# One layer of two attentions and two rotation blocks: earlier loads in the prologue, shared coupling products, a wider output projection

## The chip, the cores and the metric

The kernel runs on one core of a Trainium2 chip. The metric is the device time of one execution in microseconds (us); the time shown for the kernel before is the median of three runs. The engines are PE (TensorE), DVE (VectorE), ACT (ScalarE), POOL (GpSimd) and SP (SyncE, which here only issues DMAs). Each engine works through its own queue in order.

## What is computed

The input `x` is 2 batches of 2048 tokens with 256 features, all in float32. Four residual steps follow each other, each on the layer norm of what came before:

```python
x = x + attn_a(layernorm(x))   # 16 query heads of 16, 4 key heads, softmax over 2048 keys, projection Wo, bias bo
x = x + ffn(layernorm(x))
x = x + attn_b(layernorm(x))   # linear attention with a causal mask, rotary positions and a gate
x = x + ffn(layernorm(x))
```

The `ffn` is three cycles of a rotation, whose strength a small network computes for each token:

```python
gf = global_net(x.mean(axis=1))                    # one number for each batch
for _ in range(3):
    tf = sigmoid(gelu(gelu(gelu(out @ w1 + b1) @ w2 + b2) @ w3 + b3) @ w4 + b4)   # 256 -> 256 -> 128 -> 64 -> 1
    coupling = 0.1 + adaptive_range * (0.7 * gf + 0.3 * tf - 0.5) * 2.0
    out = out + coupling * twist(out)              # twist: [p_r, -p_i, -o_r, o_i] of the four quarters
```

## The kernel before

The 4096 tokens are eight blocks of 512 (`BLK`), four for each batch. `xs` holds all tokens with the tokens on the partitions; `zq` holds features on the partitions.

**Prologue of attention a** (lines 487 to 606). `arrive(j)` (L251) asks on SP's queue for block j of `x`. `look(j)` (L262) takes its statistics on DVE and its scale on POOL; `spread(j)` (L282) normalizes it, some of its four token tiles on DVE and the rest on ACT; `features(j)` (L293) turns it on PE and evacuates the two halves by DVE or ACT, as its argument says; `keys(j)` (L306) projects keys and values (`pk`), splits the keys into a rounded part and a rest (`kh`, `kl`), writes both to DRAM (`dk`, L244) and fetches them back spread over the partitions (`a_kP`, L249); `values(j)` (L322) turns the values (`pv`); `asked(j, m)` (L333) projects queries (`pq`); `project(u)` (L349) sends the queries of unit u through DRAM in the same way (`dq`, `qP`). `biases` (L196) gathers the key and query biases with small matmuls. `WARM` idle matmuls stand at the start.

**The maxima.** A unit is a block of queries and one of four groups, 32 in all. The generator `largest` (L362) finds each query's largest score: a step is one score matmul `s` (L376) and one DVE reduction `mx` (L380), 64 steps to a unit. After a unit's last step four small DVE operations build a row (`mr`), which goes to DRAM and back on SP's queue (`dm`, L398, then `a_m`, L403). The prologue runs the first `LEAD` = 80 steps, between which the pieces of work for the remaining blocks stand: one piece at each third step (`pieces`, L572; 22 pieces and an end). The tiles `s` have three PSUM banks of their own; in unit 0 some use the four banks of the pool `p`, which pieces and scores use too.

**The loop** (L617) has 512 iterations of a unit and 128 keys: four scores `p` (L625), four matmuls that add the maximum's row (L629, "shift"), four exponentials on ACT (L633), four `av` matmuls of the iteration before (L612), and four steps of `largest`. `finish(u)` (L445) is a generator that brings a unit's result through DRAM to `oc` in small steps; after a block's last group it projects it, one token tile at a time (`po`, L483), and adds it to `xs` (L484). `norm(j)` (L410) normalizes and turns blocks 0 to 2 for the first rotation within the loop.

**Order.** A scheduler may rearrange the instructions of an engine where no dependency forbids it. `in_order` (L136) pins the program's order on the engines that it is given: on all five for the prologue (L606), and again for everything behind attention a (L1362). The loop between is not pinned.

**Rotations** (L742). Blocks go in pairs k (12 pairs: three cycles of four): `first(k, e)` is the layer `q1` of block e of the pair, `second(k)` is `q2`, `third(k)` is `q3` (one block on each half of the partitions), `fourth(k)` applies the rotation. In the last cycle (k of 8 and more) `fourth` calls `back` (L831): the couplings are computed with the tokens on the partitions (`q4`, L839, eight matmuls with one column each; then `cf`, L844 to L846, once for each block), the features are turned (`trf`, L858), added to `xs` (L862), and the rotation's products are added too (L870); in the second rotation each half block is then stored. `rounds` (L1161) interleaves neighbouring pairs.

Of the kernel before, what the change touches and what calls it, by code (L numbers as in the profile page):

```python
# [67 lines left out]
def tile_hybrid(ctx: ExitStack, tc: tile.TileContext, x: bass.AP, consts: bass.AP, wa_d: bass.AP, wf_d: bass.AP, wb_d: bass.AP, out: bass.AP):  # L68
# [84 lines left out]
    def attention_a():  # L153
        with ExitStack() as st:
# [26 lines left out]
            def bank(name):  # L181
                return banks[0](name)
# [13 lines left out]
            def biases(raw, at, bqr, sel):  # L196


                pb = psp.tile([P, BLK], F32, tag="p", name="a_pbias")
                rows, bv = sel[:, 0:64], sel[0:1, 64:P]  # L200
                compact(rows, ident, nc.scalar.copy)
                compact(bv, raw[0:1, at["bv"][0] : at["bv"][1]], nc.scalar.copy)
                mm(pb[0:64, 0:1], rows, raw[:, at["bk"][0] : at["bk"][1]], start=True, stop=True)
                mm(pb[64:P, 0:1], bv, ones[0:1, 0:1], start=True, stop=True)
                pq = psp.tile([P, BLK], F32, tag="p", name="a_pbq")
                for e in range(2):
                    mm(pq[64 * e : 64 * e + 64, 0:2], rows, bqr[:, e::2], start=True, stop=True)
                nc.vector.tensor_copy(bkv, pb[:, 0:1])
                nc.vector.tensor_copy(bq, pq[:, 0:2])
# [52 lines left out]
            def look(j):  # L262

                st = own.tile([P, 4, 6], F32, tag="ln_st", name=f"st_a{j}", bufs=4)
                mv = own.tile([P, 4, 2], F32, tag="ln_mv", name=f"mv_a{j}", bufs=4)
                rs, nb = (own.tile([P, 4], F32, tag=f"ln_{t}", name=f"{t}_a{j}", bufs=4) for t in ("rs", "nb"))
                for t in range(4):
                    if t == 3:
                        yield
                    nc.vector.bn_stats(st[:, t, :], xs[:, 4 * j + t, :])  # L270
# [139 lines left out]
            def norm(j):  # L410

                zt = later_pools["late"].tile([P, 4, D], F32, tag="zt", name=f"zt0_{j}")
                yield from normalize_slowly(zt, j)
                if j == 2:
                    first_norms.append(zt)
                    return
                for c in range(2):
                    yield
# [26 lines left out]
            def finish(u, av):  # L445
# [60 lines left out]
            arrive(2)  # L506
            arrive(3)
# [23 lines left out]
            list(two)  # L531
# [3 lines left out]
            list(three)  # L535
            first()
            second = keys(1, ld)
            second()
            arrive(BPB)
# [7 lines left out]
            third()  # L547
            next(ahead)
# [6 lines left out]
            project(1)()  # L555
            nc.sync.dma_start(small[:, P : _CONST["ones"][0]], consts[:, P : _CONST["ones"][0]])
# [3 lines left out]
            for j in range(BPB + 1, NB):  # L560
                arrive(j)
# [10 lines left out]
            def pieces():  # L572

                memsets()
                list(look(4))
# [8 lines left out]
                for j in range(BPB, NB):  # L584
                    features(j, ld, 0)
                    if j + 1 < NB:
                        list(look(j + 1))
# [29 lines left out]
            for u, kb in ((u, kb) for u in range(len(units)) for kb in range(KB)):  # L617
                qP, mrow = queries[u], mrows[u % 2]
# [80 lines left out]
    def behind(tail):  # L699
# [41 lines left out]

        def rotations(n, part, store):  # L742
            alphas, plains = {}, {}
            acts, narrow = {}, {}
# [32 lines left out]
            def first(k, e):  # L777
# [3 lines left out]
                for m in range(2):  # L781
                    q1 = bank(f"q1f{n}_{k}_{e}_{m}")
# [5 lines left out]
            def second(k):  # L788
                narrow[k] = []
                for e in range(2):  # L790
# [6 lines left out]
                    narrow[k].append(a2)  # L797

# [31 lines left out]

            def back(k, js, a3, between):  # L831


                both = []
                for e in range(2):
                    row = slice(64 * e, 64 * e + 64)
                    q4 = bank(f"q4f{n}_{k}_{e}")
                    for tile in range(4):
                        mm(  # L839
                            q4[:, tile : tile + 1], a3[row, tile * P : (tile + 1) * P], w4[row, 0:1],  # L840
                            start=True, stop=True,
                        )
                    tt = take("small", [P, 3, 4], f"cf{n}_{k}_{e}")
                    nc.scalar.activation(tt[:, 2, :], q4[:, 0:4], AF.Tanh, bias=hb4, scale=0.5)  # L844
                    nc.vector.tensor_scalar(tt[:, 0, :], tt[:, 2, :], plain, plains[js[e] // BPB], ALU.mult, ALU.add)
                    nc.vector.tensor_scalar(tt[:, 1, :], tt[:, 0, :], -1.0, None, ALU.mult)  # L846
                    both.append(tt)
                for e in range(2):
                    j, cs, z = js[e], both[e], blk(zq, js[e])
                    if e == 1 and between:  # L850
                        between()
                    for h in range(2):
                        tr = bank(f"trf{n}_{k}_{e}_{h}")
                        for q in range(2):
                            at = slice((2 * h + q) * P, (2 * h + q + 1) * P)
                            for c in range(2):
                                to = q * D + (1 - c) * P
                                nc.tensor.transpose(tr[:, to : to + P], z[:, c, at], ident)  # L858
                        tr = tr.rearrange("p (q s f) -> p q s f", q=2, s=2)
                        half = tokens(j)[:, 2 * h : 2 * h + 2, :].rearrange("p q (s f) -> p q s f", s=2)  # L860
                        for s in range(2):
                            nc.vector.tensor_tensor(half[:, :, s, :], half[:, :, s, :], tr[:, :, 1 - s, :], ALU.add)  # L862
                        for q in range(2):
# [5 lines left out]
                            for m, quarters in enumerate((slice(0, 4, 3), slice(1, 3))):  # L869
                                nc.vector.scalar_tensor_tensor(  # L870
                                    x4[:, quarters, :], t4[:, quarters, :], cs[:, m, tile : tile + 1],
# [9 lines left out]
            return context, first, second, third, fourth  # L881
# [279 lines left out]
        def rounds(f, n):  # L1161

            context, first, second, third, fourth = f
# [15 lines left out]
        context, first, second, third, fourth = f  # L1179
# [97 lines left out]
        context, first, second, third, fourth = f  # L1277
# [82 lines left out]
        for n in range(8, 27):  # L1360
            rounds(f, n)
        in_order(begin)  # L1362
# [119 lines left out]
```

## Time and profile before

| what | value |
|---|---|
| median of three runs | 2176.52 us (2175.12 to 2176.97) |
| the profiled execution, its time | 2173.25 us |
| its span, first to last instruction | 2171.5 us |
| mean granted clock of PE | 0.992 of full |
| prologue: first `s`, first `av` of the loop | 28.99 us, 114.36 us |
| the loop, first to last `av` | 114.36 to 1554 us |
| first rotation, with the seam to attention b | 1554 to 1742 us |
| attention b and the second rotation up to its last cycle | 1742 to 2119 us |
| last DVE product, end of span | 2168.4 us, 2171.5 us |

The page of a profile lists the busy time of each engine, and the chain of work that ended last, followed back from the last instruction. A timeline lists instructions in order of time, merged: start, duration, engine, line, operation, output and inputs, and in square brackets the engine's idle time before, with what ended it. A table by stretches gives each engine's busy time and, behind the engines, the granted clock (PEclk, 1.00 is full speed), the DMA engines' busy share and GB/s. Fp32 matmuls appear as two records ("passes") each.

### The profile page before, as it was taken

How to read it: one execution, taken by the hardware profiler on the slowest of the kernel's cores; microseconds unless marked ns; L12 is line 12 of the kernel's file. 1: busy time of each engine (PE TensorE's matmuls, PEld its weight loads, DVE VectorE, ACT ScalarE, POOL GpSimd, SP SyncE). 2: the span in 40 equal slices, each digit the busy share in tenths (PEclk: the TensorE clock that was granted, in tenths of full speed). 3: DMA queues.
4: the chain of work that ended last, by engine and by line, in shares of the span. 5: the costliest groups of instructions: out<-in, count | busy, mean ns of one | idle time of the engine just before them, and what ended most of it. 6: DMA issues, size and time to landing. Idle time of an engine off the chain costs nothing.

```text
span 2171.5 us, 38896 instructions
## 1 busy us (share of the span) xinstructions
PE 2120.0 (98%) x14218; PEld 1019.6 (47%) x14218; DVE 1730.8 (80%) x3351; ACT 1417.8 (65%) x2748; POOL 348.8 (16%) x318
## 2 busy tenths in 40 slices
PE   8899999999999999999999999999999999999998
PEld 3344444444444444444444444444443567676334
DVE  5899998998999899899899899987144688876435
ACT  3377777777776777777677677778864445454442
POOL 3100000000001000000000000000145345541550
PEclk9999999999999999999999999999999999999999
DMA  6510110101101011010110101100100000000002
GB/s 179 146 54 15 40 36 17 46 12 46 36 17 46 10 48 36 17 46 12 47 36 17 37 19 48 36 17 7 51 1 0 1 1 2 1 2 1 0 1 78
DMA packets 59696, 68.73 MB, mean 32 GB/s; under 512 B 24944, under 2 KB 34032, under 8 KB 59248
## 3 DMA queue, kind: packets, MB, share of 16 engines
q1 hardware_dynamic: 58592, 64.79, 10.9%
q8 instruction: 112, 1.84, 0.3%
q10 hardware_dynamic: 720, 0.92, 0.1%
q14 instruction: 80, 0.66, 0.1%
q0 software_dynamic: 192, 0.52, 0.1%
HBM read 35.78 MB, written 26.21 MB: 29 GB/s over the span
## 4 chain that ended last, share of the span: by engine, by line
PE 85%; DVE 9%; DMA 2%; ACT 2%; issue 1%; SPq 1%; POOL 1%; ACTq 0%; DVEq 0%; POOLq 0%
PE av L612 21%; PE s L376 19%; PE p L625 10%; PE q1f L784 8%; PE p L629 6%; DVE mx L380 6%; PE q2f L794 4%; PE pe L1072 2%; PE po L483 2%; PE bpo L1098 1%; PE pv L942 1%; PE pw L942 1%; PE pq L933 1%; PE q3f L804 1%; PE pk L933 1%
## 5 line engine op out<-in xcount | busy, mean ns | idle before, releaser
L380 DVE TENSOR_REDUCE mx<-s 128x1 f32<-128x512 f32 x2048 | 1270.6, 681 | 104.1 <-PE s L376 102.5
L633 ACT ACTIVATE e<-p 128x512 f32<-128x512 f32 x2048 | 1058.8, 603 | 362.2 <-PE p L629 347.1
L376 PE MATMUL s<-a_kP,qP 64*128 64x512 f32 x2048 | 709.6, 471 | 26.9 <-DVE mx L380 24.4
L629 PE MATMUL p<-a_m,a_pick 64*128 64x512 f32 x2048 | 591.5, 416 | 0.0
L376 PEld LDWEIGHTS s<-a_kP,qP 64*128 64x128 f32 x2048 | 283.9, 184 | 588.9 <-DVE mx L380 563.4
L612 PE MATMUL av<-e,a_v 128*32 128x512 f32 x4096 | 547.2, 606 | 0.0
L625 PE MATMUL p<-qP,a_kP 64*128 64x512 f32 x2048 | 528.9, 393 | 2.0 <-ACT e L633 2.0
L625 PEld LDWEIGHTS p<-qP,a_kP 64*128 64x128 f32 x2048 | 286.4, 185 | 61.5 <-ACT e L633 26.4
L629 PEld LDWEIGHTS p<-a_m,a_pick 64*128 64x128 f32 x2048 | 283.8, 184 | 27.7
L477 POOL TENSOR_TENSOR oc<-oc,sums 128x512 f32<-128x512 f32 x16 | 20.9, 1304 | 1226.1 <-DMA sums<-dr 1078.2
L784 PE MATMUL q1f<-zq,wf 128*128 128x512 f32 x384 | 175.5, 600 | 0.0
L612 PEld LDWEIGHTS av<-e,a_v 128*32 128x32 f32 x4096 | 81.1, 108 | 129.3 <-issue 120.6
L785 ACT ACTIVATE a1f<-q1f,wf 128x512 f32<-128x512 f32 x96 | 65.8, 687 | 99.8 <-PE q1f L784 96.4
L784 PEld LDWEIGHTS q1f<-zq,wf 128*128 128x128 f32 x384 | 70.6, 190 | 98.0 <-issue 85.5
L794 PE MATMUL q2f<-a1f,wf 128*128 128x512 f32 x192 | 89.6, 610 | 0.0
L1078 DVE TENSOR_TENSOR en<-pe,small 128x512 f32<-128x512 f32 x128 | 79.3, 681 | 12.8 <-PE pe L1072 12.6
L823 DVE TENSOR_SCALAR cf<-cf,f_beta,alphaf 128x512 f32<-128x512 f32 x32 | 33.6, 1050 | 53.8 <-ACT cf L822 53.8
L827 POOL TENSOR_TENSOR tf<-cf,zq 128x512 f32<-128x512 f32 x32 | 55.5, 1735 | 92.1 <-DVE cf L823 91.7
L796 ACT ACTIVATE a2f<-q2f,wf 128x512 f32<-128x512 f32 x48 | 32.7, 686 | 55.0 <-PE q2f L794 55.0
L829 POOL TENSOR_TENSOR zq<-zq,tf 128x512 f32<-128x512 f32 x32 | 56.8, 1774 | 3.1 <-DVE tf L826 0.7
L794 PEld LDWEIGHTS q2f<-a1f,wf 128*128 128x128 f32 x192 | 35.2, 193 | 45.3 <-issue 44.4
L828 DVE TENSOR_TENSOR zq<-zq,tf 128x512 f32<-128x512 f32 x32 | 22.1, 692 | 36.1 <-POOL tf L827 36.0
(205 smaller groups left out, 1634.9 us busy)
## 6 DMA issues: line engine op xcount, KB each, us to landing
qP<-dq SPq DMA_DIRECT2D x64, 256.0 KB
dq<-qh SPq DMA_DIRECT2D x62, 128.0 KB
dq<-ql SPq DMA_DIRECT2D x62, 128.0 KB
a_kP<-dk SPq DMA_DIRECT2D x16, 256.0 KB
oc<-avs SPq DMA_DIRECT2D x128, 32.0 KB
sums<-dr SPq DMA_DIRECT2D x128, 32.0 KB
out<-xs SPq DMA_DIRECT2D x16, 256.0 KB
xs<-in_x SPq DMA_DIRECT2D x7, 512.0 KB
```

Of the source, the lines that this page charges most:

```text
L376: mm(s, qP[r // 2][row, qi * P : (qi + 1) * P], kP[r // 2][row, k0 + kb * BLK : k0 + (kb + 1) * BLK], start=True, stop=True,)
L380: nc.vector.tensor_reduce(mx[:, r, qi : qi + 1, kb], s, AX.X, ALU.max)
L612: mm(av[32 * r : 32 * r + 32, :], vA[:, units[u][0] // BPB * KB + kb, 32 * r : 32 * r + 32], es[r], start=(kb == 0), stop=(kb == KB - 1),)
L625: mm(t[r], kP[r // 2][row, k0 : k0 + P], qP[r // 2][row, :], start=True, stop=False)
L629: mm(t[r], pick[row, :], mrow[r // 2][row, :], start=False, stop=True)
L633: nc.scalar.activation(es[r], t[r], AF.Exp, scale=1.0 / HD**0.5)
L784: mm(q1, w1[:, c, m * P : (m + 1) * P], z[:, c, :], start=(c == 0), stop=(c == 1))
L785: nc.scalar.activation(a1[:, m, :], q1, AF.Gelu, bias=b1[:, m : m + 1])
L794: mm(q2, w2[:, c, :], a1[:, c, :], start=(c == 0), stop=(c == 1))
L827: nc.gpsimd.tensor_tensor(t1, cs, z[:, 0, :], ALU.mult)
L829: nc.gpsimd.tensor_tensor(z[:, 1, :], z[:, 1, :], t1, ALU.subtract)
L1078: nc.vector.tensor_tensor(self.ens[t][w], pes[w].rearrange("p (h n) -> p h n", h=4), const("triu").unsqueeze(1).to_broadcast([P, 4, P]), A ...
```

## The change

It edits these places:

- Loads: blocks 2, 3 and 4 are asked for at the start instead of 2 and 3; block 5 after the fetch of the first queries, block 6 after the fetch of block 2's keys, block 7 after the second unit's queries. Before, block 4 came after block 1's keys and 5 to 7 after two loads of constants.
- Start: six idle matmuls instead of four; the biases' matmuls and copies move behind block 0's normalization, block 0's two halves are both evacuated by ACT, and `look` is no longer split.
- `LEAD` is 74, and six more steps (`MORE`) stand in the loop's first twelve iterations, one in each second. The pieces stand at each third step up to step 52, none from 53 to 63, and the last five at steps 64 to 72.
- PE's order is pinned from the prologue through the loop's iteration (0, 3); the other four engines as before.
- The projection takes two token tiles into one PSUM bank and adds 512 columns at once. `norm` turns both halves of a block in one step.
- In `back` one set of four matmuls with two columns (`w4_pair`, zero where the other block's rows are) gives the couplings of both blocks of a pair, with one tanh and one pair of scalings.
- At the very end pair 10's `fourth` stands between the two halves of `first(11, 1)`, and pair 11's turns and plain additions behind each half of `second(11)`; `fourth(11)` then only adds the products.

```diff
+                yield
...
-                    if t == 3:
-                        yield
...
+                yield
                 for c in range(2):
-                    yield
                     tr = bank(f"ztr0_{j}_{c}")
...
-                    for t in range(4):
-                        po = bank(f"po{j}_{t}")
-                        for h in range(2):
-                            mm(po[:, 0:D], oc[:, h, t * P : (t + 1) * P], wo[:, h, :], start=(h == 0), stop=(h == 1))
-                        nc.vector.tensor_tensor(xs[:, 4 * j + t, :], xs[:, 4 * j + t, :], po[:, 0:D], ALU.add)
+                    for i in range(2):
+                        po = bank(f"po{j}_{i}")
+                        for t in range(2):
+                            tok = slice((2 * i + t) * P, (2 * i + t + 1) * P)
+                            for h in range(2):
+                                mm(
+                                    po[:, t * D : (t + 1) * D], oc[:, h, tok], wo[:, h, :],
+                                    start=(h == 0), stop=(h == 1),
+                                )
+                        pair = tokens(j)[:, 2 * i : 2 * i + 2, :]
+                        nc.vector.tensor_tensor(pair, pair, po.rearrange("p (t d) -> p t d", t=2), ALU.add)
                         yield
...
-            LEAD, WARM = 64 + 16, 4
+            LEAD, MORE, WARM = 64 + 10, 6, 6
...
-            arrive(2)
-            arrive(3)
+            for j in range(2, 5):
+                arrive(j)
...
-            list(look(0))
-            biases(raw, at, bqr, sel)
-            one, two, three = look(1), look(2), look(3)
-            next(one)
+            look(0)
+            picked = biases(raw, at, bqr, sel)
+            next(picked)
             spread(0, ld, 2)
-            next(one)
-            features(0, ld, 1)
+            features(0, ld, 0)
+            look(1)
+            next(picked, None)
...
             first()
+            arrive(5)
             second = keys(1, ld)
             second()
-            arrive(BPB)
...
             third()
+            arrive(6)
...
             project(1)()
+            arrive(7)
...
-            for j in range(BPB + 1, NB):
-                arrive(j)
...
-                if n % 3 == 1:
+                if (n % 3 == 1 and n < 55) or (n > 63 and n % 2 == 0):
                     next(rest, None)
-            in_order(begin, (engines.PE, engines.DVE, engines.Activation, engines.Pool, engines.SP))
+            in_order(begin, (engines.DVE, engines.Activation, engines.Pool, engines.SP))
...
+                if (u, kb) == (0, 4):
+                    in_order(begin, (engines.PE,))
...
+                if kb % 2 == 1 and u * KB + kb < 2 * MORE:
+                    next(ahead)
...
+            def turn_ahead(k, e):
+                for h in range(2):
+                    turned[k, e, h] = turn_back(k, e, h)
...
+                q4 = bank(f"q4f{n}_{k}")
+                for tile in range(4):
+                    mm(
+                        q4[:, 2 * tile : 2 * tile + 2], a3[:, tile * P : (tile + 1) * P], w4_pair,
+                        start=True, stop=True,
+                    )
+                cs = take("small", [P, 3, 8], f"cf{n}_{k}")
+                nc.scalar.activation(cs[:, 2, :], q4[:, 0:8], AF.Tanh, bias=hb4, scale=0.5)
+                nc.vector.tensor_scalar(cs[:, 0, :], cs[:, 2, :], plain, plains[js[0] // BPB], ALU.mult, ALU.add)
+                nc.vector.tensor_scalar(cs[:, 1, :], cs[:, 0, :], -1.0, None, ALU.mult)
...
+                        half, tr = turned.pop((k, e, h), None) or turn_back(k, e, h)
...
-        for n in range(8, 27):
+        for n in range(8, 23):
             rounds(f, n)
+        third(10)
+        first(11, 1, lambda: fourth(10))
+        second(11, lambda e: turn_ahead(11, e))
+        third(11)
+        fourth(11)
```

`turn_back` is the old body of `back`'s inner loop up to the two additions of L862: four transposes into a bank and two DVE additions.

More of the change, by code (lines that the diff above doesn't have):

```diff
@@ L416, in norm @@
                     return
+                yield
                 for c in range(2):
-                    yield
                     tr = bank(f"ztr0_{j}_{c}")
@@ L530, in attention_a @@
             features(1, ld, 0)
-            list(two)
+            look(2)
             asked(0, 0)
@@ L534, in attention_a @@
             spread(2, ld, 2)
-            list(three)
+            look(3)
             first()
+            arrive(5)
             second = keys(1, ld)
             second()
-            arrive(BPB)
             values(0)
@@ L574, in pieces @@
                 memsets()
-                list(look(4))
+                look(4)
                 values(3)
@@ L586, in pieces @@
                     if j + 1 < NB:
-                        list(look(j + 1))
+                        look(j + 1)
                     yield
@@ L740, in behind @@
         nc.vector.tensor_scalar(beta, plain, sign, None, ALU.mult)
+        w4_pair = hold.tile([P, 2], F32, name="f_w4_pair")
+        nc.gpsimd.memset(w4_pair, 0.0)
+        for e in range(2):
+            row = slice(64 * e, 64 * e + 64)
+            nc.gpsimd.tensor_copy(w4_pair[row, e : e + 1], w4[row, 0:1])
         def rotations(n, part, store):
             alphas, plains = {}, {}
-            acts, narrow = {}, {}
+            acts, narrow, turned = {}, {}, {}
             def context(b):
@@ L775, in blocks, with first @@
                 return 2 * (k % 4), 2 * (k % 4) + 1
-            def first(k, e):
+            def first(k, e, between=None):
                 z = blk(zq, blocks(k)[e])
@@ L781, in first @@
                 for m in range(2):
+                    if m == 1 and between:
+                        between()
                     q1 = bank(f"q1f{n}_{k}_{e}_{m}")
@@ L786, in first, with second @@
                 acts[k, e] = a1
-            def second(k):
+            def second(k, behind=None):
                 narrow[k] = []
@@ L797, in second @@
                     narrow[k].append(a2)
+                    if behind:
+                        behind(e)
             def third(k):
@@ L829, in fourth, with turn_back @@
                     nc.gpsimd.tensor_tensor(z[:, 1, :], z[:, 1, :], t1, ALU.subtract)
-            def back(k, js, a3, between):
-                both = []
-                for e in range(2):
[L836 to L849, printed above, removed]
+            def turn_back(k, e, h):
+                j = blocks(k)[e]
+                z = blk(zq, j)
+                tr = bank(f"trf{n}_{k}_{e}_{h}")
+                for q in range(2):
+                    at = slice((2 * h + q) * P, (2 * h + q + 1) * P)
+                    for c in range(2):
+                        to = q * D + (1 - c) * P
+                        nc.tensor.transpose(tr[:, to : to + P], z[:, c, at], ident)
+                tr = tr.rearrange("p (q s f) -> p q s f", q=2, s=2)
+                half = tokens(j)[:, 2 * h : 2 * h + 2, :].rearrange("p q (s f) -> p q s f", s=2)
+                for s in range(2):
+                    nc.vector.tensor_tensor(half[:, :, s, :], half[:, :, s, :], tr[:, :, 1 - s, :], ALU.add)
+                return half, tr
@@ new lines, in turn_ahead @@
+            def turn_ahead(k, e):
+                for h in range(2):
+                    turned[k, e, h] = turn_back(k, e, h)
+            def back(k, js, a3, between):
+                q4 = bank(f"q4f{n}_{k}")
[8 more added lines that the diff above has]
+                nc.vector.tensor_scalar(cs[:, 1, :], cs[:, 0, :], -1.0, None, ALU.mult)
+                for e in range(2):
+                    j = js[e]
@@ L852, in back @@
                     for h in range(2):
[L853 to L862, printed above, removed]
+                        half, tr = turned.pop((k, e, h), None) or turn_back(k, e, h)
                         for q in range(2):
@@ L870, in back @@
                                 nc.vector.scalar_tensor_tensor(
-                                    x4[:, quarters, :], t4[:, quarters, :], cs[:, m, tile : tile + 1],
+                                    x4[:, quarters, :], t4[:, quarters, :], cs[:, m, 2 * tile + e : 2 * tile + e + 1],
                                     x4[:, quarters, :], ALU.mult, ALU.add,
@@ L879, in back @@
                             )
-            return context, first, second, third, fourth
+            return context, first, second, third, fourth, turn_ahead
         sums1 = hold.tile([P, 2, NB], F32, name="sums1")
@@ L1161, in rounds @@
         def rounds(f, n):
-            context, first, second, third, fourth = f
+            context, first, second, third, fourth, _ = f
             k = n // 2
@@ L1178, in behind @@
         f = rotations(0, sums0, False)
-        context, first, second, third, fourth = f
+        context, first, second, third, fourth, _ = f
         turned, looked = first_norms, {}
@@ L1276, in behind @@
         f = rotations(1, sums1, True)
-        context, first, second, third, fourth = f
+        context, first, second, third, fourth, turn_ahead = f
         front, front1 = context(0), context(1)
```

## The prediction

> **What bounds the kernel now.** First the page's shares and chain: PE is busy 98% of the span and carries 85% of the chain that ended last, so work taken off another engine counts only where PE waits for it.
>
> ```profile
> PE 2120.0 (98%) x14218; PEld 1019.6 (47%) x14218; DVE 1730.8 (80%) x3351; ACT 1417.8 (65%) x2748; POOL 348.8 (16%) x318
> ...
> PE 85%; DVE 9%; DMA 2%; ACT 2%; issue 1%; SPq 1%; POOL 1%; ACTq 0%; DVEq 0%; POOLq 0%
> ```
>
> Then busy time by stage. In attention's loop (114 to 1551 us) PE is busy 1418 of 1437 us; its waits for `mx` come to 16 us there, for exponentials to 2. In both stretches of the last rotation cycle (1687 to 1720, 2120 to 2153) PE is busy all the time. PE stands only in the prologue, at the seam at 1726 to 1742, and at the very end. The prologue:
>
> ```profile
> core 0: us, PE busy (x) PEld busy (x) DVE busy (x) ACT busy (x) POOL busy (x), PEclk, DMA share, GB/s
> ...
> 37.60:41.62 4.02, 0.02 (x3) 0.01 (x1) 2.58 (x12) 0.30 (x1) 0.58 (x1) 0.75 0.42 147
> ...
> 58.72:62.04 3.32, 0.00 (x0) 0.00 (x1) 2.58 (x12) 0.29 (x1) 0.00 (x0) 1.00 0.95 314
> ...
> 109.28:114.36 5.08, 5.08 (x18) 3.41 (x18) 4.39 (x8) 3.59 (x7) 0.00 (x0) 0.50 0.16 60
> 102.00:108.00 6.00, 5.09 (x14) 1.87 (x12) 6.00 (x11) 0.27 (x2) 0.00 (x0) 0.99 0.80 258
> ```
>
> PE does nothing in the first two; the last two (busy ends are modelled) show PE paced by DVE's reductions, one `s` per 0.62 us, and the clock then at 0.50. The timeline tells why PE stood at 37.6: `look(4)` sits on DVE ahead of the reductions, and its block was requested late.
>
> ```profile
> 33.17 0.43 SPq L255 DMA_DIRECT2D xs<-in_x  x1
> ...
> 39.01 1.41 DVE L270 BATCH_NORM_STATS2 st_a<-xs 128x6 f32<-128x256 f32 x4 [4.58 <-DMA xs<-in_x]
> ```
>
> The same at 59.43 (3.05 us of DVE) for block 5, issued at 53.87 behind the constants. After each wait PE runs slow: four `pq` passes take 3.78 us at 42.33 against 1.98 elsewhere.
>
> The end is DVE's:
>
> ```profile
> 2158.73 1.52 PE L839 MATMUL q4f<-wf,a3f 64*128 64x1 f32 x16 [0.78 <-ACT a3f L806]
> ...
> 2160.19 1.97 PE L858 MATMUL trf<-small,zq 128*128 128x128 f32 x16
> ...
> 2160.99 0.75 DVE L862 TENSOR_TENSOR xs<-xs,trf 128x256 f32<-128x256 f32 x2
> 2161.78 1.13 DVE L870 SCALAR_TENSOR_TENSOR xs<-trf,cf,xs 128x128 f32<-128x128 f32 x4
> ```
>
> Four such groups (0.67 and 1.12 start to start, with issue 1.82 each) run from 2161.09 to 2168.36, then the last store lands.
>
> **1. The start, -3.5 us.** `spread(0)` on DVE waits behind the bias copy, which waits for `raw_bq` (landed 8.91), and behind three statistics of block 1: z of block 0 begins at 10.45 though its scale was ready at 7.85. In the new order z starts at 7.9 on DVE, and ACT's half ends at 9.26 as now. Two more idle matmuls are four more passes at 0.43, so PE is free at 7.16 + 1.7 = 8.9. Transposes end at about 9.9, bias matmuls at 10.6 (8 passes, some 0.6 us), ACT's two evacuations (0.55 start to start each) at 10.6: `pk` starts at 10.7 instead of 12.71, ends at 12.7 if its four passes take 1.98, and not the 3.48 of now. `kh` begins at 12.7 against 16.22. The chain behind it (kl, look(2), qh, ql, dq, qP) keeps its order and lengths, so the first `s` comes at 25.5 against 28.99. Bounds: 0, if the clock or `raw_bq` eats it, and -5.
>
> Its fourth load up front is 512 KB on a queue that moved 260 GB/s on average in the first 10 us: about 2 us after block 3, long before `look(4)`; the first wait is `look(2)` at 14. It is issued behind blocks 2 and 3 on SP, so it delays none of them.
>
> **2. The two waits for x, -11 us.** First: 4.02 idle plus slow passes (3.78 - 1.98, then 0.3 and 0.2) is 6.3; second: 3.32 plus 1.6 (pq 2.77 and 2.28 for 1.98, s 1.22 for 0.73) is 4.9. Each new load stands on SP behind a fetch that SP waits for anyway (issue 0.43); block 5 is issued near 24, needed by piece 7, near 45; 6 and 7 likewise have over 10 us. What is late next is PE itself: from 28.99 to the first `av` at 114.36 are 85.4 us, while its work is 5 pk and 14 pq at 1.92 (36.5), 4 tr at 1.03, 6 pv at 0.4, a_pb 0.6, 80 s at 0.22 (17.6) and two loop iterations without av (3.4): 64.6. So 20.8 us are lost, 11.2 to these waits.
>
> **3. The prologue's end, -3 us.** Six `s` leave (1.3 us of PE). Now: after the last maximum (`mr`, 98.25) the dm stores wait until 101.33 behind the fetch of block 7's keys, and the round trip from there to the first shift is 101.33 to 108.45, 7.1 us, in which PE only has `s` at DVE's pace, followed by half clock. After: pieces stop at step 52 and five remain behind step 63. Steps 53 to 63 are DVE's: 11 x 0.62 = 6.8 us, PE some 2.5 us idle past its three banks' lead. Then PE has 9.6 us of pieces (four of 1.92, tr, two pv) and ten s (2.2), 11.8, more than the 7.1 of the trip, and SP has nothing ahead of dm. With 17 pieces and their steps at the pace of 69.5 to 97.4 (2.54 each), 3.6 us before them: step 53 at 73, step 64 at 79, pieces done at 91, first av at 94.5. The stretch at DVE's pace is followed by slow clock as at 109: 1.7 to 3.4 us; I take 2.5, so av at 97 against 114.36: -17.4 for parts 1 to 3 together. Pinning PE through (0, 4) costs nothing as long as the shift finds its row; if not, up to 3 us of idle.
>
> [...]
>
> **4. Six steps in the loop, +1.5 us.** 6 x 0.25 of PE. DVE has 5 x 0.62 = 3.1 in each second iteration against PE's 2.70 + 0.25, and 2.48 against 2.70 in the others: 33.5 against 33.9 in twelve. No slack; bound up to +3.
>
> **5. Projection by pairs, -0.5 us.** PE's passes stay. Two adds of 0.37 become one of about 0.65 (L862 and L1078 rows: 0.74 for two 256-wide, 0.68 for one 512-wide): 16 x 0.1 = 1.6 us of DVE, while DVE idles 94 us for `s` there. PE's block grows from 1.06 to 2.12 us; DVE and ACT starve for it, but PE is the bound. What can move is the unpinned loop's order (norm too): the iteration at 336.97 took 5.7 instead of 2.7, because ACT's `zt` waits 1.92 for POOL ahead of exponentials and the clock falls. Bounds -4 (that goes) and +4 (one more).
>
> **6. Shared coupling products, -5 us.** `q4` of one pair is 16 passes, 1.45 us on the chain: 0.09 each. A 128-row weight load takes 190 ns against 187 for 64 rows, so eight passes cost 0.72; bound above, eight at the transposes' 0.119, 0.95. Saved 0.5 to 0.73, on PE, at five pairs where PE is the bound (first rotation 8 to 10, second 8 and 9): -3.6. At the seam (pair 11 of the first) the chain runs over L845, L846, L845, L846 in 3.43 us (1736.87 to 1740.35), halved: -1.5. The new column tile is three small POOL operations in attention's end, where POOL is idle.
>
> **7. The end, -3.5 us.** With pair 10's products ahead of half of `first(11, 1)`, DVE finishes pair 10 at 2156.3 (now 2158.8); its adds for pair 11 (4 x 0.74) run to 2159.3, beside q3, a3 and q4. PE's q3 still ends near 2157.9; a3 0.7, q4 0.75 less, tanh and one pair of `cf`: DVE free at 2160.3. Then 16 products at 0.28 = 4.5: 2164.8 against 2168.36. Seven PSUM banks hold it: the last early transpose needs pair 10's last bank at 2156.4, free at 2156.3. If that is late, 1 us goes; bounds -1 and -4.5.
>
> **Sum.** -17.4 + 1.5 - 0.5 - 5 - 3.5 = -25. Against the profiled run (2173.25, span 2171.5) that is 2148; it stood 3.3 under the median of the three runs, 2176.52, so I forecast 2151.
>
> [...]
>
> **Rivals.** (a) The prologue gives only its loads: the start gains 0, the quiet steps 53 to 63 cost two slow windows and DVE paces the rest. Parts 1 to 3 give -9: 2160. For it: PE and DVE both have about 45 us of work in steps 0 to 52, so either can block; against: 69.5 to 97.4 runs at 26.9 of 27.9 PE-busy. (b) The loads come early but don't help, as the prologue then waits for the key planes' trip through DRAM (SP's waits there: 17.6 us for dk): the 11 and 3 us return, and the loop eats 4: within 0.2% (4.4 us, about what a measurement of this kernel can tell from no change), near 2174. Against: kP(1) lands near 33 and is needed near 39. (c) Slower: the scheduler places ACT's or DVE's pieces around the wider projection ahead of exponentials, as at 336.97, 3.0 us each. It decides from (25 + 4.4)/3, ten such iterations; at two in each of seven blocks, 14, the time is 2176.5 + 42 - 25 = 2193. For it: one instance now; against: total ACT waits of PE are 2 us.
>
> **Numbers.** Forecast 0.72, (a) 0.16, (b) 0.07, (c) 0.05. The forecast's terms end at -34 (-22, +1.5, -4, -5, -4.5) and at -6 (-9, +3, +4, -3.5, -1) if all fall one way; the range, 2142 to 2163, takes in the first and (a), and leaves out (b), (c) and the worst joint ends, under 2 in 10. Faster 0.88, same 0.07, slower 0.05.
>
> **What would show it.** First `s` near 25.5; no DVE wait for xs past 10 us; first `av` near 97, with half clock shortly after step 63; q4 at 8 passes; last DVE product 4.5 us after the last cf. Wrong would be: an `av` after 105, iterations of over 5 us in the loop, or PE waiting for a bank near the end.

## The result, and the profile after

The changed kernel takes 2159.26 us (median of five runs, 2158.62 to 2163.14); the kernel before took 2175.71 us beside it on the same chip. The ratio is 0.9931 with an interval of 0.9917 to 0.9946. The profiled execution took 2159.26 us, with a span of 2157.5 us against 2171.5. The forecast was 2151. The change is faster, but by less than expected: 14.0 us between the profiled spans and 16.5 between the medians, where 25 were forecast.

The page's shares of engines and of the chain that ended last have hardly moved, so nothing new bounds the kernel as a whole:

```profile
PE 2111.9 (98%) x14158; PEld 1017.9 (47%) x14158; DVE 1722.7 (80%) x3318; ACT 1416.1 (66%) x2741; POOL 349.1 (16%) x321
...
PE 85%; DVE 9%; issue 2%; ACT 1%; DMA 1%; SPq 1%; POOL 1%; ACTq 0%; DVEq 0%; POOLq 0%
```

So the two executions are compared by stage, between starts of the same instruction in the two timelines:

| stage | before | after | difference | forecast |
|---|---|---|---|---|
| up to the first `s` (part 1) | 28.99 | 26.20 | -2.8 | -3.5 |
| first `s` to first `av` (parts 2, 3) | 85.37 | 80.87 | -4.5 | -13.9 |
| the first 12 iterations of the loop (part 4) | 33.22 | 37.48 | +4.3 | +1.5 |
| 13th `av` to the first `q1` (part 5) | 1406.6 | 1403.3 | -3.3 | -0.5 |
| shared products: three pairs, seam, two pairs (part 6) | | | -2.3, -1.6, -1.4 | -3.6 and -1.5 |
| the end from pair 9's `q4`, without pair 9's share of part 6 (part 7) | | | -3.5 | -3.5 |
| between two `q4` around 2020, scatter of half clock | 17.1 | 18.4 | +1.3 | none |

The sum is -13.8, and the spans differ by 14.0. Most of what is missing (9.4 of 11 us) is in one row, the prologue behind its first `s`. The stretches of the changed kernel's prologue, in the table by stretches:

```profile
core 0: us, PE busy (x) PEld busy (x) DVE busy (x) ACT busy (x) POOL busy (x), PEclk, DMA share, GB/s
26.20:46.48 20.28, 19.78 (x60) 7.72 (x60) 14.64 (x32) 7.21 (x13) 5.03 (x11) 1.00 0.61 186
46.48:56.12 9.64, 9.47 (x34) 4.16 (x33) 9.29 (x23) 1.90 (x4) 0.00 (x0) 1.00 0.78 240
56.12:60.44 4.32, 0.00 (x2) 0.01 (x1) 0.00 (x0) 0.00 (x0) 0.81 (x3) 0.77 0.46 106
60.44:69.94 9.50, 8.11 (x21) 4.16 (x21) 6.02 (x17) 4.65 (x9) 3.53 (x5) 0.57 0.33 91
...
82.37:88.27 5.90, 3.91 (x14) 1.72 (x13) 5.90 (x11) 1.00 (x2) 0.48 (x1) 0.79 0.63 153
88.27:102.40 14.13, 14.13 (x44) 6.26 (x44) 8.45 (x17) 3.85 (x7) 1.26 (x1) 0.85 0.22 50
```

Up to 56 PE idles for 0.7 us in all: the old wait at 37.6 is gone. Then PE, DVE and ACT stand for 4.32 us and POOL for most of it. PE takes 9.50 us for what follows, since the granted clock is 0.57 and ACT and POOL are late; the same instructions take 4.88 in experiment 3 below, where nothing holds them (55.29 to 60.17). The wait and these 4.6 us more are 8.9 together. The row at 82.37 is the quiet steps 53 to 63 at DVE's pace, with slow clock behind them, as forecast. PE's timeline names who ended the wait:

```profile
55.66 0.46 PE L325 MATMUL pv<-small,kv 64*128 64x64 f32 x4
60.44 1.22 PE L226 MATMUL a_pb<-a_db,small 128*128 128x256 f32 x2 [4.32 <-POOL a_db L221]
61.59 1.38 PE L374 MATMUL s<-a_kP,qP 64*128 64x512 f32 x3
64.36 1.97 PE L131 MATMUL tr<-small,z 128*128 128x128 f32 x8 [1.39 <-ACT zq L341]
```

`a_pb` spreads the projection's bias over a row: a piece of the prologue (`rows`) loads the eight slices of `wo` and the bias `a_bo`, POOL builds `a_db` from it, and two small matmuls follow. POOL's and SP's timelines of the same stretch:

```profile
59.63 0.75 POOL L221 TENSOR_TENSOR a_db<-small,a_bo 128x128 f32<-128x128 f32 x2 [22.83 <-DMA a_bo<-in_wa]
60.34 1.01 POOL L273 TENSOR_TENSOR rs_a<-rs_a,small 128x4 f32<-128x4 f32 x1
```

```profile
53.47 4.35 SPq L216 DMA_DIRECT2D a_wo<-in_wa  x8
57.87 0.42 SPq L217 DMA_DIRECT2D a_bo<-in_wa  x1
```

The load of 1 KB for which PE stands is issued behind eight loads whose data are first used at 314.8, and their issue alone takes SP 4.35 us. POOL had been idle for 22.83 us with `a_db` at the head of its queue; the scale of the next block (L273) stood behind it, which is why ACT's `zq` and then `tr` are late too. Before the change the same load was issued later still, and PE did not wait for it:

```profile
62.92 0.42 SPq L216 DMA_DIRECT2D a_bo<-in_wa  x1
```

```profile
68.91 0.70 PE L225 MATMUL a_pb<-a_db,small 128*128 128x256 f32 x2
```

POOL built `a_db` at 64.74 there. PE had stood for block 5 of `x` until 62.04 and had two `pq` and a `pv` to do before it came to `a_pb`.

Two more views answer to what the prediction showed. At the start `pk` of block 0 now runs at full speed, 1.98 us, at 11.16 instead of 12.71:

```profile
8.29 1.45 PE L517 MATMUL idle<-still 128*128 128x512 f32 x3
9.57 1.04 PE L131 MATMUL tr<-small,z 128*128 128x128 f32 x8
...
11.16 1.98 PE L308 MATMUL pk<-zb,a_wkv 128*128 128x512 f32 x4
```

At the end DVE's timeline shows pair 11's additions (L863) ahead of its couplings and behind them only the 16 products, where additions and products took turns before:

```profile
2145.84 2.73 DVE L863 TENSOR_TENSOR xs<-xs,trf 128x256 f32<-128x256 f32 x8
2149.74 0.29 DVE L881 TENSOR_SCALAR cf<-cf,f_plain,plainf 128x8 f32<-128x8 f32 x1 [1.17 <-ACT cf L880]
2150.06 0.17 DVE L882 TENSOR_SCALAR cf<-cf 128x8 f32<-128x8 f32 x1
2150.14 4.22 DVE L896 SCALAR_TENSOR_TENSOR xs<-trf,cf,xs 128x128 f32<-128x128 f32 x16
```

### The profile page after: what moved, and what is told of

Its sections match the earlier page's. It is cut to its first block, busy times and chain, and to the rows that moved or that the text cites. A ratio compares the mean times of both kernels' runs of the same rounds, so it can differ in the third digit from the quotient of the medians.

```text
span 2157.5 us, 38739 instructions
## 1 busy us (share of the span) xinstructions
PE 2111.9 (98%) x14158; PEld 1017.9 (47%) x14158; DVE 1722.7 (80%) x3318; ACT 1416.1 (66%) x2741; POOL 349.1 (16%) x321
## 4 chain that ended last, share of the span: by engine, by line
PE 85%; DVE 9%; issue 2%; ACT 1%; DMA 1%; SPq 1%; POOL 1%; ACTq 0%; DVEq 0%; POOLq 0%
PE av L617 21%; PE s L374 20%; PE p L632 10%; PE q1f L801 8%; PE p L636 6%; DVE mx L378 6%; PE q2f L811 4%; PE pe L1098 2%; PE bpo L1124 1%; PE po L483 1%; PE pq L959 1%; PE pw L968 1%; PE pk L959 1%; PE pv L968 1%; PE q3f L823 1%
## 5 line engine op out<-in xcount | busy, mean ns | idle before, releaser
L475 POOL TENSOR_TENSOR oc<-oc,sums 128x512 f32<-128x512 f32 x16 | 20.5, 1282 | 1235.5 <-DMA sums<-dr 1086.6
```

## The experiments

Ratios are to the kernel before on the same chip. The first four kernels ran on one chip, the next four on another, and the last four together on that one. "The early bias" is one edit, in either kernel: `a_bo` is asked for at the start, on ACT's queue.

```diff
             nc.scalar.dma_start(bqr, wa_d[:, slice(*_WA["bq"])])
+            nc.scalar.dma_start(bo, wa_d[:, slice(*_WA["bo"])])
...
-                nc.sync.dma_start(bo, wa_d[:, slice(*_WA["bo"])])
                 yield
```

**1. The loads alone.** The kernel before with the new places of the loads of `x`, and nothing else.

```diff
-            arrive(2)
-            arrive(3)
+            for j in range(2, 5):
+                arrive(j)
...
+            arrive(5)
...
-            arrive(BPB)
...
+            arrive(6)
...
+            arrive(7)
...
-            for j in range(BPB + 1, NB):
-                arrive(j)
```

> The kernel before with the new places of the x loads alone (blocks 2 to 4 at the start, 5, 6 and 7 behind three fetches). Theory A: the two waits for x go (11.2 us by the forecast), but the bias vector a_bo, which stands on SP behind eight loads of wo, is then late in their place: in the changed kernel POOL's a_db waits for it until 59.63, PE's a_pb 4.32 us, and the clock is slow behind that, 8.9 us in all. So the gain is 11.2 - 8.9, about 2 us (0 to 4), 2174, and PE shows a wait of over 3 us for a_db. Theory B (the forecast's part 2): the loads alone give 11 us, 2165, and no such wait.

Measured: 2174.25 us, ratio 0.9984 (0.9975 to 0.9993). Both waits for `x` are gone, and PE's timeline has the new one in full:

```profile
65.44 1.22 PE L225 MATMUL a_pb<-a_db,small 128*128 128x256 f32 x2 [5.28 <-POOL a_db L220]
```

The first `av` comes at 114.65 against 114.36. So the two waits, 7.3 us of PE's idle time, are gone, and the prologue ends no earlier: the next wait and the slow clock behind it took their place. Theory B falls; the 2 us (0 to 4) of theory A fit, with 3.5 by the ratio.

**2. The loads and the early bias, in the kernel before.** Experiment 1 with the edit above.

> As the run with the x loads alone, and a_bo is asked for at the start on ACT's queue. Theory A: now the whole 11.2 us come, 2164 to 2166, with no wait of PE for a_db. Theory C: a_bo is only where the wait shows, and the prologue is held by the key planes' trips through DRAM or by DVE; then the time stays within 2 us of the run with the loads alone and another wait of PE of the same size appears.

Measured: median of ten runs 2175.17 us, ratio 0.9974 (0.9963 to 0.9985), but in two groups: two runs near 2167, the profiled one among them (2167.51), eight between 2173.5 and 2175.9. In the trace the wait for `a_db` is gone and the first `av` comes at 103.09. But the time is not theory A's 2164 to 2166: the median is within 1 us of experiment 1's, as theory C has it, though PE waits nowhere longer than 1.8 us up to 120. What eats this gain was left for experiment 12.

**3. The early bias in the changed kernel.**

> The changed kernel with a_bo asked for at the start on ACT's queue, nothing else. Theory A: 7 to 9 us under the changed kernel (4.32 idle, some 4.6 of slow clock): about 2151, first av near 98 to 100 instead of 107.06. Theory C: under 3 us, 2157 or more, first av at 104 or later.

Measured: 2149.71 us, ratio 0.9871 (0.9857 to 0.9884), an interval that lies wholly below the changed kernel's own. The wait is gone in PE's timeline:

```profile
54.90 0.46 PE L324 MATMUL pv<-small,kv 64*128 64x64 f32 x4
55.29 0.70 PE L225 MATMUL a_pb<-a_db,small 128*128 128x256 f32 x2
55.92 0.72 PE L373 MATMUL s<-a_kP,qP 64*128 64x512 f32 x3
```

The first `av` stands at 97.26, where the prediction had put it (97). One load of 1 KB, moved, takes 10.2 us off the span (2147.3 against 2157.5). Some 3 of them may be scatter, since half clock also lasted 3.4 us instead of 6.8 behind the quiet steps and again around 2010; by the ratios the gain is 0.6%, 13 us. Theory A is shown: the wait is gone, and the size is no less than it expected.

**4. The six extra steps in pairs.** The changed kernel, with two extra steps in each of iterations 3, 7 and 11.

```diff
-                if kb % 2 == 1 and u * KB + kb < 2 * MORE:
+                if kb % 4 == 3 and u * KB + kb < 2 * MORE:
                     next(ahead)
+                    next(ahead)
```

> The changed kernel with the six extra steps of the loop in three pairs (iterations 3, 7 and 11) instead of one in each second iteration. From first av to the thirteenth the changed kernel takes 37.48 us, the kernel before 33.22: 0.71 us for each extra step where 0.25 was forecast. Theory D: one extra step shifts the order of the row halves (0, 1, 1, 0 by 64 rows), so the s that go together are then on the same half and no longer run side by side; two steps keep the order, cost about 0.25 each, and the loop's start gets 2 to 3 us shorter: 2156 to 2157. Theory E: DVE is the bound (five reductions of 0.62 against 2.70): six reductions in one iteration cost as much, the time stays within 1 us of 2159.

Measured: 2164.45 us, ratio 0.9929 (0.9916 to 0.9941), like the changed kernel's 0.9931; the kernel before took longer on this chip as well (2178.3 us). The twelve iterations take 37.50 us, against 37.48. An iteration with two extra steps takes 3.90 to 4.13 us; in the timeline of all engines DVE has six reductions on end, and ACT waits for the scores behind them:

```profile
128.29 3.68 DVE L378 TENSOR_REDUCE mx<-s 128x1 f32<-128x512 f32 x6 [0.22 <-PE s L374]
...
129.86 2.07 ACT L640 ACTIVATE e<-p 128x512 f32<-128x512 f32 x4 [1.67 <-PE p L636]
```

The price of an extra step in the loop is 0.7 us, near DVE's 0.61 for a reduction and not PE's 0.25, whether the steps come singly or in pairs. Theory E holds.

**5. The shared products alone**, in the kernel before: `w4_pair` and the `q4` and `cf` of the diff in front.

> The kernel before with the shared coupling products alone. Forecast's part 6: 0.5 to 0.73 us of PE at each of six pairs in which PE is the bound (first rotation 8 to 10, second 8 to 10), 1.5 us at the seam, and half a microsecond at the end (one pair of cf less): -5 to -6 us. Rival: PE's gain is given back as a wait for the exponentials' or DVE's side of the pair (a2, bank releases), under 2 us. In the trace: 14.86 us from q4 to q4 of neighbouring pairs becomes 14.1 to 14.3.

Measured: 2170.98 us, ratio 0.9967 (0.9956 to 0.9979). In the first rotation the steps from `q4` to `q4` shrink from 14.9, 14.9 and 15.8 us to 14.1, 14.1 and 15.0, the stretch with the seam by 1.1, pair 8 of the second rotation by 0.8, and from pair 9's `q4` to the end of the last product 34.03 become 32.14. The sum is -6, as expected.

**6. The old projection and `norm`** in the changed kernel: one token tile at a time, and `norm` in two steps.

```diff
-                    for i in range(2):
+                    for t in range(4):
...
-                yield
                 for c in range(2):
+                    yield
                     tr = bank(f"ztr0_{j}_{c}")
```

> The changed kernel with the projection one token tile at a time and norm's turns in two steps again, as before. From the loop's thirteenth av to the first q1f the changed kernel takes 3.3 us less than the kernel before. Theory F: this is the projection and norm (fewer DVE instructions, ACT's z of norm placed better: the iterations of 4.5 to 4.8 us that follow the projection are 3.9 in the changed kernel); then this run is 2 to 4 us slower than the changed kernel, 2161 to 2163. Rival: it is scatter of the loop's order; then it is within 1.5 us of 2159 and the loop takes 1403 us as in the changed kernel.

Measured: 2164.51 us, ratio 0.9941 (0.9927 to 0.9956), which overlaps the changed kernel's own. By stage it is clearer: from the 13th `av` to the first `q1` 1407.8 us against 1403.3. Single iterations tell where: a projection adds 4.44 us to four iterations (3.77, 3.94, 3.77, 3.76) against 4.27 to two (4.87, 4.80), and the iteration of the `norm` behind it takes 4.51 instead of 3.86. So pairing the token tiles saves 0.2 us in each of the first three blocks of the seven; in the four others it is 0.06 (15.06 against 15.00). Turning a block in one step rather than two saves 0.65 in each of three, with 0.15 more in the iterations after two of them (3.73 once instead of 3.29 twice, where 2.70 is usual). That explains about 3.1 of the 4.5 us; the rest is spread over many iterations. It isn't scatter between executions: from the 13th `av` to the first `q1` the seven traces with the old projection and `norm` take 1406.2 to 1410.4 us, the seven with the new ones 1403.3 to 1404.7. Theory F holds.

**7. Early bias, 80 steps in the prologue, none extra in the loop**, the last pieces three steps apart.

```diff
-            LEAD, MORE, WARM = 64 + 10, 6, 6
+            LEAD, MORE, WARM = 64 + 16, 0, 6
...
-                if (n % 3 == 1 and n < 55) or (n > 63 and n % 2 == 0):
+                if n % 3 == 1 and not 54 < n < 64:
```

> The changed kernel with a_bo early, and the six steps back in the prologue (80 steps, none extra in the loop), the last five pieces three steps apart from step 64. In the loop the six cost 4.3 us (DVE's pace, 0.7 each). Behind step 63 DVE is busy only 8.45 of 14.1 us, so theory G expects them nearly free there: PE 6 x 0.22 = 1.3; the loop's first twelve iterations take 33.2 again, so 3 us less than the run with a_bo early alone, 2146 to 2147. Rival: DVE's turn comes behind PE's pieces and the six add 6 x 0.62 = 3.7 before the loop; then no gain, 2149 to 2151.

Measured: 2147.68 us, ratio 0.9863 (0.9846 to 0.9880). The twelve iterations take 33.06 us, 4.4 less than in experiment 3; the first `av` comes at 100.45, 3.2 later, with 6.8 us of half clock instead of 3.4. So the six steps cost 4.4 us in the loop and about 1.5 ahead of it, if the 1.7 us for the longer half clock are set apart. The time lies between theory G's and the rival's; it can't be told from experiment 3's, as the two intervals overlap.

**8. Early bias, and a piece at each third step all along**, as in the kernel before.

```diff
-                if (n % 3 == 1 and n < 55) or (n > 63 and n % 2 == 0):
+                if n % 3 == 1:
```

> The changed kernel with a_bo early, and the pieces at each third step all along (none left out from 53 to 63). Theory H: the quiet stretch costs PE 1.8 us of waiting and, through the slow clock behind it (four pq passes 3.78 for 1.98), as much again; even pieces save 2 to 3.5: 2146 to 2147, first av 94 to 95 where the run with a_bo early has 97.26. Rival: the trip of the maxima's row (7.1 us from dm to the first shift) is then covered by two pieces and ten s only; PE waits in iteration 0 instead, and the first av stays at 97 or comes later.

Measured: 2150.6 us, ratio 0.9880 (0.9863 to 0.9897). By time it can't be told from experiment 3. The first `av` comes at 98.88, later than in experiment 3 (97.26), and PE waits 1.4 us for the first row (`a_m`), as the rival has it. Theory H falls. Whether holding pieces back for the row's trip pays isn't shown: the 13th `av` is 1.8 us later (136.58 against 134.77), but half clock lasts 6.8 us here and 3.4 there, which alone makes 1.7.

**9. Early bias, and the end in the old order.** The shared products stay.

```diff
-        for n in range(8, 23):
+        for n in range(8, 27):
             rounds(f, n)
-        third(10)
-        first(11, 1, lambda: fourth(10))
-        second(11, lambda e: turn_ahead(11, e))
-        third(11)
-        fourth(11)
```

> The changed kernel with the bias loaded at the start, but with the end in the old order: pair 10's products after all of first(11) and pair 11's turns and additions behind its couplings (the shared couplings stay). Theory (part 7 of the prediction): the new order of the end is worth about 4 us, all of it behind k = 9 of the second rotation: 2153 to 2154, against 2149.7 with the new order. Rival: DVE's additions are only moved, the last product is late anyway: within 1 us, 2150 to 2151.

Measured: 2156.61 us (2151.98 to 2158.14), ratio 0.9889 (0.9870 to 0.9908). The median stands 7 us above experiment 3's. The traced execution is its slowest, with a span 9.1 us longer, and little of that is at the end: from pair 9's `q4` to the last product are 32.13 us, against 29.88 in experiment 3. The new order is worth 2.2 us, where the expectation said 4: the shared products, by experiment 5, have the other 1.9 of the 4.2. Of the rest 1.3 is half clock around 2017 (6.8 us for 3.4), and 5.5 stand ahead of the loop, in code that is the same in both: the first `av` comes at 102.73 instead of 97.26. The table by stretches shows why, first for experiment 3, then for this one:

```profile
74.00:78.00 4.00, 2.47 (x9) 0.89 (x7) 4.00 (x8) 0.29 (x1) 0.00 (x0) 1.00 0.62 122
78.00:82.00 4.00, 3.90 (x7) 1.41 (x7) 3.86 (x10) 0.00 (x0) 0.00 (x0) 0.57 0.32 116
82.00:86.00 4.00, 4.00 (x21) 2.22 (x20) 2.69 (x5) 2.02 (x4) 0.00 (x0) 1.00 0.04 7
```

```profile
78.00:82.00 4.00, 3.10 (x5) 1.37 (x6) 3.96 (x8) 0.00 (x0) 0.00 (x0) 0.62 0.36 131
82.00:86.00 4.00, 4.00 (x12) 1.75 (x11) 2.03 (x7) 0.99 (x2) 0.00 (x0) 0.50 0.03 4
86.00:90.00 4.00, 4.00 (x11) 2.41 (x11) 1.76 (x3) 1.17 (x2) 0.00 (x0) 0.50 0.02 4
90.00:94.00 4.00, 4.00 (x7) 1.28 (x6) 0.49 (x2) 0.69 (x1) 0.00 (x0) 0.67 0.00 0
```

The clock (the number before the last two) falls at 79 in both, behind the quiet steps. In the one it is back after 3.4 us, in the other after 13.7.

**10. The early bias alone**, in the kernel before.

> The kernel before with one change alone: the output bias is loaded at the start. Theory A (in the kernel before, the waits for blocks 4 and 5 of x hide the late bias): nothing to gain, 2173 to 2176, a ratio within 0.999 to 1.001, with both waits of DVE for x near 37 and 59 as before. Rival: the late bias held the kernel before as well: 3 us or more, a ratio below 0.9985.

Measured: 2174.9 us, ratio 0.9986 (0.9977 to 0.9995), between the two expectations. The trace, of an execution of 2176.19 us, speaks for theory A: the first `av` comes at 114.33 (before 114.36), and PE still waits for the reductions that stand behind the two late blocks of `x`:

```profile
41.57 0.49 PE L375 MATMUL s<-a_kP,qP 64*128 64x512 f32 x1 [3.78 <-DVE mx L379]
...
61.98 0.79 PE L375 MATMUL s<-a_kP,qP 64*128 64x512 f32 x1 [4.01 <-DVE mx L379]
```

Where the median's 3.5 us would come from no stage shows; the kernel before varied from 2173.92 to 2184.88 on that chip. By time it is inconclusive.

**11. Early bias, 80 steps in the prologue, the last pieces two steps apart.** As experiment 7, without its second line.

> The changed kernel with the bias at the start and 80 steps in the prologue, none extra in the loop; the last five pieces stay two steps apart (64 to 72), so steps 73 to 79 stand alone at the end. Theory (a step ahead of the loop costs PE 0.22 where pieces run beside it, and DVE's 0.62 where none do): first av at 99 to 101 against 97.3, twelve iterations in 33.1 instead of 37.5, 2147 to 2149. Rival: the end of the prologue runs at DVE's pace and the clock halves behind it as in the kernel before: first av at 103 or later, 2152 or more.

Measured: 2150.81 us, ratio 0.9869 (0.9852 to 0.9887). The trace is of the slowest of its five runs (2155.57): first `av` at 106.5, with 13.7 us of half clock from 79 on and 3.4 more at 102. Neither expectation is met cleanly: the place is the rival's, the time nearly the theory's. Experiments 3, 7, 8 and 11 have overlapping intervals; which of them is best isn't told apart.

**12. Experiment 2 once more**, for a second trace.

> The same kernel as the one with new load places and early bias, for one more trace: its times fell at 2167 and at 2175. Theory (slow-clock windows in the prologue and the first iterations, more or longer ones in the slower executions): if this trace is of the slower value, the 8 us stand ahead of the 13th iteration as windows at half clock. Rival: they stand elsewhere, in the rotations or the last store. If it is of the faster value, nothing is told apart.

Measured: 2171.07 us in one run, 3.6 above the first trace and between the two groups. Up to the first `av` the two executions agree (102.94 and 103.09). The stretches behind it, of experiment 2 and then of this one:

```profile
95.00:105.00 10.00, 10.00 (x20) 4.21 (x20) 8.26 (x14) 1.20 (x2) 0.00 (x0) 0.50 0.48 172
105.00:115.00 10.00, 10.00 (x52) 3.90 (x54) 4.12 (x7) 6.43 (x13) 0.00 (x0) 0.99 0.01 2
```

```profile
95.00:105.00 10.00, 9.97 (x20) 4.14 (x20) 8.11 (x14) 1.19 (x2) 0.00 (x0) 0.50 0.44 160
105.00:115.00 10.00, 10.00 (x18) 2.86 (x20) 0.00 (x0) 3.26 (x6) 0.00 (x0) 0.50 0.00 0
```

From one `av` to the next, with a score and a shift between them, PE takes 1.63 us in the one (105.90 to 107.53) and 3.00 in the other (106.36 to 109.36). Half clock lasts 10.2 us in the one and 20.5 in the other, which is 5.1 us of work; the second unit's row is then 4.6 us later (142.8 against 138.2). So one program gives two times because the clock comes back earlier or later. It also tells what became of much of experiment 2's gain. At the first `av` the two executions are some 11 us ahead of the kernel before (114.36). At the 13th, 5.4 and 0.8 are left (142.18 and 146.74 against 147.58): the first iterations take longer here, the more so the longer half clock lasts. The runs near 2175 have no trace; that they have still longer stretches of half clock is likely, not shown.

## Why the prediction was right and wrong

**Part 1, the start (-3.5, measured -2.8).** Right in mechanism and nearly in size: `pk` starts at 11.16, where 10.7 was forecast, and takes the 1.98 us on which the sum rested, against 3.48 before. Which of the start's changes brings the full clock isn't shown.

**Part 2, the waits for `x` (-11).** The waits went, as forecast. What failed is the sentence after it: "What is late next is PE itself". It counted PE's work and the loads' slack, and never asked what else among the pieces waits for a DMA. The next late thing was `a_bo`, 4.32 us of wait and 8.9 in all with the slow clock and POOL's queue behind it. In the trace of before one could have seen it: SP issued it at 62.92, PE was to use it at 68.91, and with a shorter start and two waits gone the piece that uses it comes up 12.8 us sooner (56.12), its load only 5.0 (57.87). The sign that the prediction named for itself, a first `av` after 105, came at 107.06. Experiment 1 shows it taking the place of the gain. Experiment 3 shows that without it the prologue of the changed kernel ends where it was forecast. The 11.2 us themselves were not seen in the kernel before: loads and early bias together gave it 5.7 by the ratio (experiment 2), as the first iterations behind its old prologue took much of the gain back (experiment 12).

**Part 3, the prologue's end (-3).** Right once the bias is out of the way: 97.26 in experiment 3 against 97. That it came so close is in part luck, since the same code gave 102.73 in experiment 9. "Pinning PE through (0, 4) costs nothing" was not tried by itself. The 2.5 us for slow clock behind the quiet steps lies low in what turned out to be a spread: 1.7 us of work lost in experiment 3, 3.4 in the changed kernel, 6.8 in experiment 9.

**Part 4, the extra steps (+1.5, measured +4.3).** Mis-sized, beyond the bound of +3: the sum took PE's 0.25 for each step and read DVE's 33.5 of 33.9 us as room. With five reductions an iteration takes 3.3 to 3.5 us instead of 2.70, and the next, with four, doesn't catch up: a step costs 0.7, about DVE's own pace (experiment 4). The room was counted over twelve iterations, but is there only within one.

**Part 5, the projection (-0.5, measured -3.3, and 4.5 in experiment 6).** Mis-sized: the projection itself saves about 0.9 us over the seven blocks, and `norm` in one step, which the sum had at nothing and only the bounds took in, some 2.2.

**Parts 6 and 7 (-5 and -3.5, measured -5.3 and -3.5).** Right, by counting records and their durations: `q4` is eight records in 0.95 us where it was sixteen in 1.52, and a pair gains 0.76, a little above the 0.5 to 0.73 forecast. The last product ends 4.1 us behind the last `cf`, forecast 4.5. Of the end's 3.5 us the new order has 2.2 (experiment 9); the remaining 1.3 are pair 10's and 11's share of the shared products.

```profile
2124.48 0.95 PE L875 MATMUL q4f<-f_w_pair,a3f 128*128 128x2 f32 x8
2136.87 0.95 PE L875 MATMUL q4f<-f_w_pair,a3f 128*128 128x2 f32 x8
```

**The rivals.** (a) had the right number, 2160, mostly for another reason: the slow clock that it set behind the quiet steps came (6.8 us at 0.50), but the start did gain, and the bias, not DVE's pace, held the prologue. (b) saw rightly that the loads could come early and not help, as in experiment 1, but PE never waited for the key planes' trip. Its sum doesn't come out either: 2176.5 - 25 and the 11, 3 and 4 us that it gives back are 2170, not 2174. (c) fell: each of the seven blocks has two long iterations, as it feared, but of 4.8 us each (from `av` to `av`), and they stand in place of four of 3.8.

## What to carry to other kernels

When a stall is taken out, go through everything that the stalled engine does in the time after it, and for each operand ask when its load was issued and behind what: a load that was late all along shows no wait while another wait covers it. Put small operands that are needed early ahead of bulk loads that are needed late, on whatever queue is free. And a step given to an engine's loop costs that of the engine which has the least room within one iteration, not on average over several: here 0.7 us, with DVE's reduction at 0.61 and PE's part at 0.25.

## What the runs showed of the hardware

**The same code, nearly the same gaps, another length of slow clock.** Near the prologue's end the clock fell to 0.50. It stayed there for 3.4 us in experiment 3, 6.8 in the kernel before, in the changed kernel and in experiments 7 and 8, 10.2 in experiment 2, 13.7 in experiments 9 and 11, and 20.5 in experiment 12: each within 0.1 of a multiple of the shortest. PE's busy time ahead of it doesn't tell the length: it was 2.47, 2.85, 2.83 and 3.36 of the 4 us from 74 to 78 in experiments 3, 7, 11 and 9, and the half clock 3.4, 6.8, 13.7 and 13.7. In experiment 12 PE was busy for all of 105 to 115, by its modelled ends, and the clock stayed at half. What decides isn't shown. Between the two executions of experiments 2 and 12 this made 5.1 us of work, about what the shared products gained.

**Half clock behind short gaps.** Half clock followed the quiet steps at 79. In experiment 3 PE was busy 2.47 of the 4 us from 74 to 78, so that all its gaps together are 1.53, and the clock was 0.57 from 78 to 82. In the prediction's row at 102 they are 0.91 of 6 us, and the clock was 0.50 from 109.28 to 114.36.

**Full speed soon behind transposes.** In all eight traces with the new start `pk` of block 0 took 1.98 us behind its eight transposes (1.04 us in the changed kernel, with 0.6 us of the biases' matmuls between); in the six with the old start it took 3.48 to 3.78, 3.48 in the kernel before, where the clock was 0.50 from 12.4 to 15.6. The old start has two idle matmuls fewer, in the kernel before PE waits 1.4 and 1.7 us ahead of the transposes, and the biases' matmuls stand ahead of them; which of these makes the difference was not tried.

**Issue time on SP's queue.** Eight loads of 32 KB took SP 4.35 us to issue in the changed kernel, 0.8 of it a wait for a load of `x`, and 7.42 in the kernel before with 2.9 us of such waits. The 1 KB load that PE stood 4.32 us for was queued behind them.
